# Two depthwise convolutions moved from VectorE to TensorE in the opening of a conv-attention kernel

## The chip, the cores and the metric

The kernel runs on one core of one Trainium2 chip, in one launch, in f32. The metric is the time of one execution on the device in microseconds (us); lower is better. The core has TensorE (PE; weight loads are shown apart as PEld), VectorE (DVE), ScalarE (ACT), GpSimd (POOL) and SyncE (SP, which here only issues DMAs), and 16 DMA engines.

## The reference, cut to what matters

Eight images of 384 channels and 32 x 32 positions pass through two layers. The first normalises each position over its channels, and feeds the result to a selective state-space scan (16 states, forwards and backwards over the 1024 positions) and to a local branch. The second is causal attention with 6 heads and a feed-forward part with binarized weights. The change touches two depthwise convolutions of the first layer: a causal one of 4 taps on one half of the input projection, once in each direction, and a 3x3 one on the normalised image.

```python
xn = rmsnorm(x, norm_w)                        # over channels
u, z = split(xn @ in_proj_w.T)
uc = causal_depthwise_conv(u, conv1d_w)        # 4 taps; once forwards, once on the flipped sequence
u  = silu(uc + conv1d_b)
dt, Bm, Cm = split(u @ x_proj_w.T)
delta = softplus(dt @ dt_proj_w.T + dt_proj_b)
h[t] = exp(delta[t] * A) * h[t-1] + delta[t] * u[t] * Bm[t]     # 384 channels x 16 states
y[t] = sum_n(h[t] * Cm[t]) + u[t] * D ;  y *= silu(z)
conv  = depthwise_conv_3x3(xn, dw_w)           # padding 1
local = sigmoid(conv + dw_b) * xn
x = x + res_scale * (scale_mod * out_proj(y_fwd + y_bwd) + local)
```

## The kernel before, in words

Channels lie on the 128 partitions, in NC = 3 blocks `c`; the 1024 positions lie along the free dimension and are worked on in two halves `h` of 512, which is one PSUM bank. The stages of an image are `before_scan` (everything up to the operands of the scan), the scan itself, and `attention` with `feed_forward`. Images are taken in ORDER = 0, 1, 2, 3, 5, 6, 4, 7.

**before_scan.** It loads the image into `xn` (one of six buffers of the pool `big`, each 3 x 1024 f32 a partition), normalises it (L329), and then, for each channel block: `in_proj` makes `up` and `z` (24 matmuls, L336, copied out at L343); `conv` makes the causal convolution in a PSUM bank, forwards and backwards and for both halves: ACT writes the first tap (L352), DVE adds three more, each as one `scalar_tensor_tensor` that multiplies a shifted view of `up` with a column of `vec` (the weights, one column a tap) and adds it in place (L362), and ACT adds the bias on the way out to `u` (L363); the step `gates` makes the 3x3 convolution with `local`, in two PSUM banks: ACT writes the middle tap (L373), DVE adds eight (L383), each on a window of the picture (31 or 32 columns by 15 or 16 rows). In `gates` ACT then runs silu over `u` and `z` (L423) and tanh over the two banks (L442), with loads of its function tables around them (L446 and others); this order on ACT is pinned. DVE forms the local branch (L449, L452) and the sum of both directions (L427). `project` multiplies `u` with the small weights (L476, L487). After the third block, 12 `delta` steps make the scan's operands (L507 on PE, L510 to L513 on ACT, L514 to L517 on DVE) and write them to memory. For image 0 alone `gates` is cut in two: silu of `u` stays in place, the local branch goes to a list of later steps.

**The scan.** 768 units, 96 an image, each of two states of one block, direction and half. A unit runs through `s_row` (loads of the rows of B and C broadcast over the partitions, tile `bc`), `s_first` (POOL multiplies into `g`, L564; seven buffers), `s_scan` (ACT makes the decay `da`, L577, two PSUM banks; DVE scans, L582, two instructions; POOL keeps the carry, L587, and multiplies with C, L588) and `s_sum` (PE adds up the states by eight transposing matmuls, L598, into one PSUM bank `y`). `s_gate` ends a half of a block (L625 to L640). `s_first` runs two units ahead of `s_scan`, `s_sum` one behind it.

**The order.** The steps of the stages carry weights in us; `spread_over` interleaves lists of steps in proportion to them, and that is the program order. A scheduler then sets the order on each engine ahead of time, by priority and by what is ready; each engine runs its queue in that order. At the start `before_scan` of image 0 runs alone (`begin`). Then the 96 units of image 0 (`first`) run beside the list `beside`: the local branch of image 0, `before_scan` of image 1, the binarizing of `w1` and `w2` (loads into `big`, L205; L223 to L254), and `before_scan` of images 2 and 3. Everything up to there is called the opening here. After it the remaining units run beside attention and feed-forward of one image after the other (its first product is L667), and `before_scan` of the last four images stands beside feed-forward. PSUM has eight banks: `y` 1, `da` 2, `s` 2, `pt` 2, `av` 1; `before_scan` takes its banks from `s` and `pt` in turn.

Of the kernel before, what the change touches and what calls it, by code (L numbers as in the profile page):

```python
# [11 lines left out]
AF = mybir.ActivationFunctionType  # L12
ALU = mybir.AluOpType
# [4 lines left out]
P = 128  # L18
B, C, H, W = 8, 384, 32, 32
L = H * W  # L20
NC = C // P
# [5 lines left out]
DCONV = 4  # L27
# [16 lines left out]
ORDER = (0, 1, 2, 3, 5, 6, 4, 7)  # L44
# [3 lines left out]
V_NORM, V_CW, V_CB, V_DTB, V_D, V_DW, V_DWB, V_BP, V_B2, V_ALOG = 0, 1, 5, 6, 7, 8, 17, 18, 19, 20  # L48
# [4 lines left out]
def kernel(  # L53
# [16 lines left out]
    nc = tc.nc  # L70
# [32 lines left out]
    def half(h):  # L103
        return slice(h * HB, (h + 1) * HB)
# [23 lines left out]
    vec = ctile("vec", [P, NC, NV])  # L128
# [25 lines left out]
    ident = ctile("ident", [P, P])  # L154
# [147 lines left out]
                    )  # L302


    def before_scan(b, tags, emit, later=None):

        st = {}
        turns = itertools.cycle(tags)

        def bank_of(name):  # L310
            return bank(name, next(turns))
# [33 lines left out]
        def conv(c, d, h):  # L345

            acc = bank_of(f"u{d}_{b}_{c}_{h}")
            up = st["up", c]
            for s in range(DCONV):
                w = vec[:, c, V_CW + DCONV - 1 - s : V_CW + DCONV - s]  # L350
                if s == 0:
                    nc.scalar.activation(acc, up[:, half(h)], AF.Copy, scale=w)  # L352
                    continue
                lo, hi = h * HB, (h + 1) * HB
                if d == 0:
                    t0, t1 = max(lo, s), hi
                    tap = up[:, t0 - s : t1 - s]
                else:
                    t0, t1 = lo, min(hi, L - s)
                    tap = up[:, t0 + s : t1 + s]  # L360
                to = acc[:, t0 - lo : t1 - lo]
                nc.vector.scalar_tensor_tensor(to, tap, w, to, ALU.mult, ALU.add)  # L362
            nc.scalar.activation(  # L363
                st["u", d, c][:, half(h)], acc, AF.Identity, bias=vec[:, c, V_CB : V_CB + 1]
            )

        def local(c, h):

            acc = bank_of(f"loc_{b}_{c}_{h}")
            r0, rows = h * (HB // W), HB // W  # L370
            img = acc.rearrange("p (i j) -> p i j", j=W)
            src = st["xn"][:, c, :].rearrange("p (i j) -> p i j", j=W)
            nc.scalar.activation(  # L373
                acc, st["xn"][:, c, half(h)], AF.Copy, scale=vec[:, c, V_DW + 4 : V_DW + 5]
            )
            for k in range(9):
                di, dj = k // 3 - 1, k % 3 - 1
                if k == 4:
# [4 lines left out]
                nc.vector.scalar_tensor_tensor(  # L383
                    to,
                    src[:, i0 + di : i1 + di, j0 + dj : j1 + dj],
                    vec[:, c, V_DW + k : V_DW + k + 1],
                    to,
                    ALU.mult,
                    ALU.add,
                )  # L390
            return acc

        def weights_of(c):
# [9 lines left out]
        for c in range(NC):  # L403
# [29 lines left out]
            def gates(c=c, silus=silus, sum_of_us=sum_of_us):  # L433
                st["xc"] = mtile(f"xc_{b}_{c}")
                load(st["xc"], x[b, chunk(c), :])
                accs = [local(c, h) for h in range(NH)]
                with tc.high_priority(offset=60):
                    us = [st["u", 0, c], st["u", 1, c]] if later is None else []
                    silus(us + [st["z", c]])
                    for h in range(NH):  # L440
                        pin(
                            nc.scalar.activation(  # L442
                                accs[h], accs[h], AF.Tanh, scale=0.5, bias=dwbh[:, c : c + 1]
                            )
                        )
                    pin(nc.scalar.preload_act_table_set(LOG_EXP))  # L446
                for h in range(NH):
                    acc, xc = accs[h], st["xc"][:, half(h)]
                    nc.vector.scalar_tensor_tensor(  # L449
                        acc, acc, 1.0, st["xn"][:, c, half(h)], ALU.add, ALU.mult  # L450
                    )
                    nc.vector.scalar_tensor_tensor(xc, acc, rsh, xc, ALU.mult, ALU.add)  # L452
# [624 lines left out]
    def steps_of(stage, *args):  # L1077
        out = Steps()
        stage(*args, out)
        return out  # L1080


# [1 line left out]
    per, ahead = len(units) // B, 3  # L1084
    first = slots(-AHEAD - 2, per + 1)
    others = slots(per + 1, len(units) + 1)
    beside = Steps()
# [85 lines left out]
```

## Time and profile before

| | |
|---|---|
| median of 10 runs | 5253.6 us (5227.14 to 5259.9) |
| profiled execution | 5256.14 us, span 5254.3 us, mean granted clock 0.865 |
| PE busy | 4173.4 us, 79% of the span, 16458 matmuls |
| DVE busy | 3562.1 us, 68% |
| ACT busy | 2725.3 us, 52% |
| POOL busy | 3669.4 us, 70% |
| DMA | 1199.86 MB, mean 228 GB/s |
| L564 and L588 on POOL | 768 each, 1827.8 and 1817.9 us |
| L383 on DVE (3x3 taps) | 384 instructions, 257.7 us, mean 724 ns |
| L362 on DVE (causal taps) | 288 instructions, 201.3 us, mean 745 ns |

The profile is one execution. Its page gives the busy time of each engine, the span in 40 equal slices (busy tenths, PE's granted clock and DMA's share), the costliest groups of instructions, and DMAs. Behind the page stand views of the trace: a timeline (start, length, engine, line, operation, output and inputs, count; in brackets the idle time before it and what ended it), waits (engine and line, what it waited for, us in total, times, the longest), and windows (busy time of each engine in a stretch). PE's busy time is modelled and overlaps in pipelined matmuls. L-numbers are lines of the kernel before.

### The profile page before, as it was taken

To read this page: it belongs to the slowest core of one execution; us is meant where nothing else is said; L and a number is where in the kernel's file an instruction comes from. 1 tells how busy PE (TensorE), PEld (TensorE's weight loads), DVE (VectorE), ACT (ScalarE), POOL (GpSimd) and SP (SyncE) were. 2 spreads that over 40 slices of the span, in tenths; PEclk is the share of its full clock that TensorE was granted. 3 is DMA by queue.
4 is the path that set the end of the run, shared out by engine and by line. 5 is a ranking of instruction groups with operands and counts; after the bars stand their busy time and mean duration, and the time that the engine had idled before them with its cause. 6 is when DMAs were issued, how large, how long until landed. Compare 5 with 4: busy or idle time off the path is not lost.

```text
span 5254.3 us, 52624 instructions
## 1 busy us (share of the span) xinstructions
PE 4173.4 (79%) x16458; PEld 2199.2 (42%) x16458; DVE 3562.1 (68%) x4249; ACT 2725.3 (52%) x4914; POOL 3669.4 (70%) x1932
## 2 busy tenths in 40 slices
PE   5465566889787888777887788888888888888899
PEld 2233233444344444434444344443444544444444
DVE  6998887667786657776677766677666665666422
ACT  4665554455653555645556445565355363454434
POOL 0477675977777877759876697867788987877700
PEclk7667676989888899889899789998889998999989
DMA  6878688757678667686676876766966866667500
GB/s 226 277 242 281 225 266 274 246 182 266 212 245 293 211 216 244 216 292 222 229 256 212 269 269 207 237 236 218 308 222 219 273 220 226 212 205 239 190 29 25
DMA packets 625121, 1199.86 MB, mean 228 GB/s; under 512 B 44440, under 2 KB 103240, under 8 KB 624840
## 3 DMA queue, kind: packets, MB, share of 16 engines
q1 hardware_dynamic: 615328, 1180.34, 67.1%
q10 hardware_dynamic: 9512, 16.15, 0.9%
q8 instruction: 130, 2.13, 0.2%
q14 instruction: 151, 1.24, 0.1%
HBM read 1030.65 MB, written 165.68 MB: 228 GB/s over the span
## 4 chain that ended last, share of the span: by engine, by line
POOL 32%; issue 20%; DVE 12%; PE 11%; DMA 8%; ACT 3%; SPq 1%; POOLq 0%; DVEq 0%; ACTq 0%
POOL g L564 18%; POOL g L588 13%; DMA bc<-rows 5%; DVE g L582 5%; PE yp L1000 2%; PE s L753 2%; DVE loc L383 1%; PE av L839 1%; DVE u L362 1%; PE y L598 1%; PE qp L697 1%; DVE dp L515 1%; PE pt L825 1%; POOL carry L587 1%; ACT h L980 1%
## 5 line engine op out<-in xcount | busy, mean ns | idle before, releaser
L564 POOL TENSOR_TENSOR g<-ud,bc 128x1024 f32<-128x1024 f32 x768 | 1827.8, 2380 | 842.9 <-PE y L598 431.8
L588 POOL TENSOR_TENSOR g<-g,bc 128x1024 f32<-128x1024 f32 x768 | 1817.9, 2367 | 318.3 <-issue 158.0
L577 ACT ACTIVATE da<-dl,amat 128x512 f32<-128x512 f32 x1536 | 1058.0, 692 | 1637.8 <-DVE g L582 1594.9
L582 DVE TENSOR_TENSOR_SCAN g<-da,g 128x512 f32<-128x512 f32 x768 | 906.4, 1211 | 560.3 <-POOL g L564 523.1
L598 PE MATMUL y<-ident,g 128*128 128x128 f32 x6144 | 965.3, 305 | 384.5 <-POOL g L588 361.1
L582 DVE TENSOR_TENSOR_SCAN g<-da,carry,g 128x512 f32<-128x512 f32 x768 | 955.7, 1272 | 424.2 <-POOL g L564 402.1
L598 PEld LDWEIGHTS y<-ident,g 128*128 128x128 f32 x6144 | 792.6, 157 | 819.9 <-POOL g L588 501.6
L753 PE MATMUL s<-k,q 64*128 64x512 f32 (+3 forms) x1152 | 461.8, 600 | 178.9 <-ACT pr L774 141.5
L773 DVE TENSOR_REDUCE nm<-s 128x1 f32<-128x512 f32 (+3 forms) x576 | 300.4, 545 | 263.9 <-PE s L762 202.1
L774 ACT ACTIVATE pr<-s,nm 128x512 f32<-128x512 f32 (+3 forms) x576 | 329.0, 574 | 150.7 <-DVE nm L773 144.0
L839 PE MATMUL av<-ptn,v 128*64 128x512 f32 (+3 forms) x1152 | 367.7, 543 | 28.8 <-DVE o L851 22.7
L955 PE MATMUL hp<-t,w 128*128 128x512 f32 x720 | 338.4, 615 | 37.9 <-DMA w<-w1s 24.4
L336 PE MATMUL in<-xn,win 128*128 128x512 f32 x576 | 296.8, 660 | 65.3 <-ACT up L343 35.6
L825 PE MATMUL pt<-ident,pr 128*128 128x128 f32 x1728 | 311.7, 305 | 35.6 <-ACT ptn L829 27.0
L1000 PE MATMUL yp<-h,w 128*128 128x512 f32 x720 | 326.5, 612 | 2.7 <-DMA w<-w2s 2.7
L829 ACT COPY ptn<-pt 128x512 f32<-128x512 f32 (+3 forms) x576 | 259.2, 479 | 127.0 <-PE pt L825 124.6
L753 PEld LDWEIGHTS s<-k,q 64*128 64x128 f32 x1152 | 161.8, 205 | 338.7 <-ACT pr L774 220.2
L825 PEld LDWEIGHTS pt<-ident,pr 128*128 128x128 f32 x1728 | 212.1, 154 | 168.1 <-ACT ptn L829 76.1
L697 PE MATMUL qp<-t,wqk 128*128 128x512 f32 x576 | 266.6, 611 | 13.6 <-DVE t L300 13.6
L383 DVE SCALAR_TENSOR_TENSOR loc<-xn,vec,loc 128x496 f32<-128x496 f32 (+3 forms) x384 | 257.7, 724 | 4.2 <-ACT loc L373 4.1
L362 DVE SCALAR_TENSOR_TENSOR u<-up,vec,u 128x512 f32<-128x512 f32 (+3 forms) x288 | 201.3, 745 | 31.5 <-ACT u L352 31.2
L955 PEld LDWEIGHTS hp<-t,w 128*128 128x128 f32 x720 | 134.8, 196 | 193.6 <-issue 151.6
(154 smaller groups left out, 4539.5 us busy)
## 6 DMA issues: line engine op xcount, KB each, us to landing
bc<-rows SPq DMA_DIRECT2D x1536, 512.0 KB, 5.1
t<-st SPq DMA_DIRECT2D x63, 512.0 KB, 6.1
su<-u SPq DMA_DIRECT2D x48, 512.0 KB, 4.6
du<-su SPq DMA_DIRECT2D x96, 256.0 KB, 5.1
sdl<-du SPq DMA_DIRECT2D x96, 256.0 KB, 2.8
sud<-du SPq DMA_DIRECT2D x96, 256.0 KB, 3.4
ud<-sud SPq DMA_DIRECT2D x96, 256.0 KB, 5.7
dl<-sdl SPq DMA_DIRECT2D x96, 256.0 KB, 5.7
```

Of the source, the lines that this page charges most:

```text
L564: pin(nc.gpsimd.tensor_tensor(g, ud, sst.pop(("bc", 0, u.name)), ALU.mult))
L577: nc.scalar.activation(da, sst["dl", u.b, u.c, u.part], AF.Exp, scale=amat[:, u.c, n : n + 1])
L582: nc.vector.tensor_tensor_scan(gi[:, ::step], da[:, ::step], gi[:, ::step], first, ALU.mult, ALU.add)
L588: pin(nc.gpsimd.tensor_tensor(g, g, sst.pop(("bc", 1, u.name)), ALU.mult))
L598: nc.tensor.matmul(out=y[:, j, :], lhsT=g[:, i, chunk(j)], rhs=ident, is_transpose=True, start=(opens and i == 0 and j == 0), stop=(closes ...
L697: nc.tensor.matmul(out=qp, lhsT=st["wqk"][:, c, o : o + P], rhs=st["xn"][:, c, half(h)], start=(c == 0), stop=(c == NC - 1),)
L753: nc.tensor.matmul(out=ss[e][:, : k1 - k0], lhsT=st["q"][rows_of(e), c, chunk(qi)], rhs=st["k"][rows_of(e), c, k0:k1], start=True, stop=(k ...
L774: nc.scalar.activation(pr, s, AF.Exp, bias=m, accum_out=rs[:, i, e, kb : kb + 1])
L825: nc.tensor.transpose(pt[:, chunk(i)], st["pr", c, g, i, e][:, chunk(j)], ident)
L839: nc.tensor.matmul(out=av[rows_of(e), cols], lhsT=st["v"][:, j, hd * HD : (hd + 1) * HD], rhs=st["ptn", j, e][:, cols], start=(j % QT == 0 ...
L955: nc.tensor.matmul(out=hp, lhsT=st["w1"][:, c, chunk(m % 2)], rhs=st["xn"][:, c, half(h)], start=(c == 0), stop=(c == NC - 1),)
L1000: nc.tensor.matmul(out=yp, lhsT=st["w2", k // 6][:, k % 6, :], rhs=st["h", k // NC][:, k % NC, half(h)], start=(k == 0), stop=(k == NF - 1),)
```

## The change

For the first four images of ORDER (all of the opening) both convolutions are done on PE. Ahead of everything, 39 diagonal matrices are made, one for each of the 13 taps and 3 channel blocks: POOL multiplies the 128x128 identity with the tap's column. They lie in two tiles of the pool `big` (eight taps fit in one), which are held until the last tap has been used. A tap is then one f32 matmul of its diagonal with the shifted view, added up in the PSUM bank that DVE used before; the whole first or middle tap opens the sum, so ACT's first write goes too. ACT still reads the bank as before. The last four images keep the old way. Nothing else is changed; numbers of buffers and the weights of the steps are the same.

```diff
-    def before_scan(b, tags, emit, later=None):
+    def before_scan(b, tags, emit, later=None, diags=None):
...
             for s in range(DCONV):
-                w = vec[:, c, V_CW + DCONV - 1 - s : V_CW + DCONV - s]
-                if s == 0:
+                k = V_CW + DCONV - 1 - s
+                w = vec[:, c, k : k + 1]
+                if s == 0 and diags is None:
                     nc.scalar.activation(acc, up[:, half(h)], AF.Copy, scale=w)
                     continue
...
-                nc.vector.scalar_tensor_tensor(to, tap, w, to, ALU.mult, ALU.add)
+                if diags is None:
+                    nc.vector.scalar_tensor_tensor(to, tap, w, to, ALU.mult, ALU.add)
+                else:
+                    nc.tensor.matmul(out=to, lhsT=diags(c, k), rhs=tap,
+                        start=(s == 0), stop=(s == DCONV - 1), skip_group_check=True)
...
-            nc.scalar.activation(
-                acc, st["xn"][:, c, half(h)], AF.Copy, scale=vec[:, c, V_DW + 4 : V_DW + 5]
-            )
-            for k in range(9):
+            if diags is None:
+                nc.scalar.activation(
+                    acc, st["xn"][:, c, half(h)], AF.Copy, scale=vec[:, c, V_DW + 4 : V_DW + 5]
+                )
+            for k in (4, 0, 1, 2, 3, 5, 6, 7, 8):
...
+                tap = src[:, i0 + di : i1 + di, j0 + dj : j1 + dj]
+                if diags is None:
+                    nc.vector.scalar_tensor_tensor(
+                        to, tap, vec[:, c, V_DW + k : V_DW + k + 1], to, ALU.mult, ALU.add)
+                else:
+                    nc.tensor.matmul(out=to, lhsT=diags(c, V_DW + k), rhs=tap,
+                        start=(k == 4), stop=(k == 8), skip_group_check=True)
...
+    taps = list(range(V_CW, V_CW + DCONV)) + list(range(V_DW, V_DW + 9))
+    where, fit = {}, L // P
+    for k in range(0, len(taps), fit):
+        t = btile(f"diag_{k}").rearrange("p c (i q) -> p c i q", q=P)
+        for c in range(NC):
+            for i, tap in enumerate(taps[k : k + fit]):
+                nc.gpsimd.tensor_scalar(
+                    t[:, c, i, :], ident, vec[:, c, tap : tap + 1], None, ALU.mult)
+                where[c, tap] = t[:, c, i, :]
+
+    def diags(c, tap):
+        return where[c, tap]
...
-    before_scan(ORDER[0], ("s", "pt"), begin, beside)
+    before_scan(ORDER[0], ("s", "pt"), begin, beside, diags)
     run(begin)
-    beside += steps_of(before_scan, ORDER[1], ("s", "pt"))
+    beside += steps_of(before_scan, ORDER[1], ("s", "pt"), diags=diags)
...
     for b in ORDER[2 : 1 + ahead]:
-        beside += steps_of(before_scan, b, ("s", "pt"))
+        beside += steps_of(before_scan, b, ("s", "pt"), diags=diags)
```

More of the change, by code (lines that the diff above doesn't have):

```diff
@@ L361, in conv @@
                 to = acc[:, t0 - lo : t1 - lo]
-                nc.vector.scalar_tensor_tensor(to, tap, w, to, ALU.mult, ALU.add)
+                if diags is None:
+                    nc.vector.scalar_tensor_tensor(to, tap, w, to, ALU.mult, ALU.add)
+                else:
+                    nc.tensor.matmul(
+                        out=to,
+                        lhsT=diags(c, k),
+                        rhs=tap,
+                        start=(s == 0),
+                        stop=(s == DCONV - 1),
+                        skip_group_check=True,
+                    )
             nc.scalar.activation(
@@ L372, in local @@
             src = st["xn"][:, c, :].rearrange("p (i j) -> p i j", j=W)
[L373 to L376 removed]
+            if diags is None:
+                nc.scalar.activation(
+                    acc, st["xn"][:, c, half(h)], AF.Copy, scale=vec[:, c, V_DW + 4 : V_DW + 5]
+                )
+            for k in (4, 0, 1, 2, 3, 5, 6, 7, 8):
                 di, dj = k // 3 - 1, k % 3 - 1
[L378 removed]
+                if k == 4 and diags is None:
                     continue
@@ L382, in local @@
                 to = img[:, i0 - r0 : i1 - r0, j0:j1]
[L383 to L390, printed above, removed]
+                tap = src[:, i0 + di : i1 + di, j0 + dj : j1 + dj]
+                if diags is None:
+                    nc.vector.scalar_tensor_tensor(
+                        to, tap, vec[:, c, V_DW + k : V_DW + k + 1], to, ALU.mult, ALU.add
+                    )
+                else:
+                    nc.tensor.matmul(
+                        out=to,
+                        lhsT=diags(c, V_DW + k),
+                        rhs=tap,
+                        start=(k == 4),
+                        stop=(k == 8),
+                        skip_group_check=True,
+                    )
             return acc
@@ L1075, in run, with steps_of @@
             f()
-    def steps_of(stage, *args):
+    def steps_of(stage, *args, **kwargs):
         out = Steps()
-        stage(*args, out)
+        stage(*args, out, **kwargs)
         return out
@@ L1086 @@
     others = slots(per + 1, len(units) + 1)
+    taps = list(range(V_CW, V_CW + DCONV)) + list(range(V_DW, V_DW + 9))
[5 more added lines that the diff above has]
+                nc.gpsimd.tensor_scalar(
+                    t[:, c, i, :], ident, vec[:, c, tap : tap + 1], None, ALU.mult
+                )
+                where[c, tap] = t[:, c, i, :]
+    def diags(c, tap):
+        return where[c, tap]
     beside = Steps()
     begin = Steps()
-    before_scan(ORDER[0], ("s", "pt"), begin, beside)
+    before_scan(ORDER[0], ("s", "pt"), begin, beside, diags)
     run(begin)
-    beside += steps_of(before_scan, ORDER[1], ("s", "pt"))
+    beside += steps_of(before_scan, ORDER[1], ("s", "pt"), diags=diags)
     beside += steps_of(binarize, w1, w1s, NC, FF, 2, "w1")
```

## The prediction, made before the changed kernel had run

> **What bounds the kernel now.** I read the page's 40 slices first, then windows of the first millisecond, then POOL's timeline, gap by gap. A slice is 131 us.
>
> ```profile
> PE   5465566889787888777887788888888888888899
> DVE  6998887667786657776677766677666665666422
> POOL 0477675977777877759876697867788987877700
> PEclk7667676989888899889899789998889998999989
> ```
>
> Over the whole run no engine is full, but the stages differ. In slices 2 to 6 DVE stands at 8 to 9 tenths and PE at 4 to 6, at a clock of 6 to 7 tenths; from slice 8 on PE has 7 to 9 tenths and DVE, but for the last, 5 to 7. The first seven slices (917 us) are about the opening that the change touches: `before_scan` of image 0 by itself, then images 1, 2 and 3 beside the scan of image 0. The windows show it in finer grain (PE, PEld, DVE, ACT, POOL, then PE's clock, the DMA share and GB/s):
>
> ```profile
> core 0: us, PE busy (x) PEld busy (x) DVE busy (x) ACT busy (x) POOL busy (x), PEclk, DMA share, GB/s
> 150.00:200.00 50.00, 10.78 (x22) 4.47 (x20) 50.00 (x78) 34.36 (x46) 5.09 (x5) 0.57 0.83 296
> 200.00:250.00 50.00, 32.18 (x98) 16.78 (x98) 45.57 (x58) 32.13 (x45) 37.14 (x21) 0.82 0.76 259
> 250.00:300.00 50.00, 32.11 (x102) 16.82 (x102) 45.63 (x55) 30.75 (x43) 40.68 (x21) 0.73 0.77 258
> 300.00:350.00 50.00, 29.66 (x106) 15.31 (x106) 42.43 (x54) 32.14 (x45) 40.50 (x24) 0.80 0.74 253
> 900.00:950.00 50.00, 43.12 (x154) 22.77 (x155) 31.69 (x33) 23.38 (x37) 46.75 (x24) 0.97 0.93 319
> ```
>
> At 150 to 200 us the scan should start; DVE is busy for all of it, POOL and PE hardly. 200 to 350 is the convolution part of image 1. The last row, just behind the opening, shows what PE, POOL and DMA can do together. Who holds POOL, which sets the pace of the scan:
>
> ```profile
> POOL carry L587 <- DVE g L582: 82.4, 8, 49.7
> 273.69 9.62 DVE L383 SCALAR_TENSOR_TENSOR loc<-xn,vec,loc 128x496 f32<-128x496 f32 x15
> 277.89 2.40 POOL L564 TENSOR_TENSOR g<-ud,bc 128x1024 f32<-128x1024 f32 x1
> 286.86 2.45 DVE L582 TENSOR_TENSOR_SCAN g<-da,carry,g 128x512 f32<-128x512 f32 x2
> 289.44 2.35 POOL L588 TENSOR_TENSOR g<-g,bc 128x1024 f32<-128x1024 f32 x1 [9.16 <-issue]
> ```
>
> One wait of 49.7 us is the scan's start: the first scan runs at 150.57 us, the second at 192.43, and between them DVE runs 32.3 us of L383, the 3x3 convolution of image 0. The other lines are the pattern of the convolution parts: a run of L383 (here 15 in a row, 9.62 us), behind it the scan of DVE, and POOL without work from 280.3 to 289.4. Between such gaps POOL repeats L588 every 4.87 us (213.67, 218.54, 223.42), which is full. There is one gap for each channel block of images 1 to 3: 8.1, 9.2, 9.3, 12.1, 6.5, 15.9, 10.3, 9.5 and 9.0 us, in sum 89.8 us. POOL's other gaps lie in the `delta` parts between (350 to 450, 590 to 660, 810 to 880), end mostly at `bc` loads, and I leave them as they are. So in this stage the wait that ends last is DVE's, and the convolutions are in it.
>
> **What a matmul costs.** PE's rows give two prices:
>
> ```profile
> 33.62 0.19 PEld L336 LDWEIGHTS in<-xn,win 128*128 128x128 f32 x1 [0.26 <-issue]
> 34.05 0.19 PEld L336 LDWEIGHTS in<-xn,win 128*128 128x128 f32 x1 [0.24 <-issue]
> 182.53 5.01 PE L261 MATMUL ms<-sq_n,onesc 128*128 128x512 f32 x6 [31.56 <-DVE xc L452]
> ```
>
> With the clock up, weight loads follow each other at 0.43 us, one for each f32 matmul of 512 columns, so a tap costs 0.43 us. After PE had idled 31.56 us, six took 5.01 us, 0.84 each. The group's mean (660 ns for L336) is not the price: the spans of matmuls that follow each other overlap.
>
> The Trainium skill, "FP8 and Floating Point Precision", TensorE Precision Notes, says that true FP32 makes four passes through the array, and "TensorE: Matmul & The Clock Gate" gives 2.4 GHz for the warm clock; as an estimate that is 512 x 4 / 2.4 GHz = 0.85 us a tap, twice the spacing in the trace, and speaks against the change: put into the sum below it makes 102 x 0.85 = 87 us of PE work an image, 161 with what is there, 191 us at the rate used there, and so 3 x 41 - 28 = 95 us lost, 5349. The trace decides, and everything else here goes by its 0.43.
>
> **The change part by part.** *Removed from DVE:* in four images 192 instructions of L383 and 144 of L362. Their busy time in the opening by windows is 126.5 and 99.2 us, so 226 us of the 736 us that DVE is busy in the first 900. *Removed from ACT:* the first tap of each sum, L373 x24 and L352 x48, 16.6 + 32.4 = 49 us.
>
> *Added to PE:* each image has 12 half rows of 4 taps and 6 half pictures of 9, so 102 matmuls; four images 408, or 408 x 0.43 = 175 us at full clock (343 us at 0.84). Does PE have room? In 200 to 350 its work in full-clock time is 32.18 x 0.82 + 32.11 x 0.73 + 29.66 x 0.80 = 73.5 us; 102 x 0.43 = 43.9 come on top, 117 us. At the rate of 900 to 950 (43.12 x 0.97 / 50 = 0.84) this takes 140 us, against 150 now. POOL's own bound for the 27 units in these 150 us is 27 x 4.87 = 131. Giving back the gaps whole would make it 120.
>
> *Sum for images 1 to 3:* so each gains 10 us if PE sets the pace, 18 if POOL does, 30 if the gaps just vanish. I take 15, between the first two because both engines would be near full and PE takes its queue in order: 45 us. The DVE work of the same steps that stays (L427, L449, L452: 3.9 us in the gap at 283 to 287) is one reason not to take more.
>
> *The scan's start:* of DVE's 50 us between 150 and 200, 32.3 are L383; PE is idle there (10.8 us busy) and can take the 54 taps of image 0 in 23 to 45 us beside it. DVE keeps the steps of `delta`, which feed the scan anyway. I take 28 us; bounds 0 (were the chain of `delta` and ACT to end as late) and 33.
>
> *Image 0's causal convolution (first 100 us).* Per channel block 16 taps, 6.9 us (13.4 cold), against 12 of L362 at 0.75 = 9 us plus 4 of ACT; but they now stand in the same queue as the input projection (11.1 us for 24). PE is idle after each projection until the silus end, so I take 0; bounds 9 us gained to 21 lost for the three blocks.
>
> *The 39 diagonals on POOL.* No row shows this form. The nearest, POOL's select on 128x128, took 0.29 us: 11 us from 8.5 us, where `vec` lands; the first tap is wanted at 36 us. Were each as long as POOL's 128x1024 product (2.36 us), the four that the first block needs would end at 18 us and the 24 of all causal taps at 65, before the third block's at 86. Cost 0; POOL has nothing else until 134 us, which is its cover.
>
> *Two of six big buffers.* The diagonals hold them until the last tap near 800 us; four are left for the pictures `xn` and for binarizing w1 and w2. The loads of `xn` for images 2 and 3 are issued at 176 and 180 us and first needed near 422 and 652, so they can wait; binarizing will stretch from 20 to 135 us into the next part, where DVE now has room. Cost 0, at most 10 us.
>
> *The new queueing.* On PE, 18 taps in a row (7.7 us, cold 15) stand ahead of the scan's y transposes L598, and those free `g`, for which POOL's L564 waits. `g` has 7 buffers and about four units are under way, so two or three units of 4.87 us cover it. A tap group also waits for a PSUM bank, and whatever stands behind it on PE waits too: now L336 waits so for L452 in 3 places, 9.6 us. I take 5 us lost; bounds 0 and 40.
>
> Sum: 28 + 45 - 5 = 68 us gained. The profiled execution took 5256.14 us (span 5254.3), 2.5 above the median, so 5256.1 - 68 = 5188 for it, and on the median 5253.6 - 68 = 5186 us. Everything behind the opening keeps its work and moves forward as a whole.
>
> **Rivals.** *Only the start is gained.* The gaps stay but change owner: POOL waits for `bc` rows (already 62.7 us in 13 waits in the opening, and 0.93 share of DMA at the pace of 900 to 950), or DVE's L449 stands in its queue for tanh, which stands for PE. Then 28 us: 5226. *Nothing measurable.* `delta`'s chain holds the start and the gaps change owner: near 5250. *Slower: PE becomes the bound of the opening.* It needs 117 us of full-clock work an image. If clock and waits leave it a rate r, that takes 117/r; with the 28 us from the start, r = 117/(150 + 9) = 0.74 is the point from which it loses. Now r is 0.49 in these parts, behind the opening 0.84. At 0.65 an image takes 180 us: 3 x 30 - 28 = 62 us lost, 5316. For it: strict order, bank waits, a clock of 0.73 to 0.87. Against it: the clock reaches 0.97 where PE has work, and the taps of a group depend on nothing new. *It does not do what it says*, if a strided picture row costs PE more than 0.43: that would show as the same loss.
>
> **How the numbers follow.** Forecast 0.58, only the start 0.19, nothing 0.07, slower 0.16. About 0.2%, 10 us, is what a measurement here can tell from no change. Faster 0.58 + 0.19 = 0.77, same 0.07, slower 0.16. The low end takes the whole start (33), all gaps (90) and 20 us of the earlier causal part and of ACT: 5110. The high end takes in the no-change case and a little more, 5262; most of the slower case is left out.
>
> **What would show it.** In the profile after: L383 and L362 only 192 and 144 times, DVE at 5 to 7 tenths and PE at 7 or more with a clock of 8 to 9 in slices 2 to 6; the wait of 49.7 us under 25; POOL's gaps at the gates under 5 us; attention's first step (L667), now at 878 us, near 810. It is wrong if the first slices show PE at 8 to 9 with POOL's waits for y at the head, if `bc` heads them, or if POOL's gaps stay near 10 us with DVE idle in them.

## The result: slower by 0.28%, and the profile after

The changed kernel took 5258.1 us (median; 5246.8 to 5267.7), against 5242.8 us for the kernel before on the same chips. The ratio is 1.0028, 95% interval 1.0017 to 1.0039: about 15 us slower. The forecast was 68 us faster. The time lies inside the range given, 5110 to 5262, and on the other side of no change. The profiled execution took 5263.27 us, its span 5261.4 us, at a mean granted clock of 0.895 (0.865 before). L-numbers below are those of the changed kernel: L367 are the causal taps on PE, L402 the 3x3 taps, L583 and L607 POOL's two products of a unit, L617 the transposing matmuls into `y`, L539 the stores of `delta`.

First the slices of the page:

```profile
PE   7897988888787888778887788888888888888899
DVE  3656557566786657776677766686766665666522
POOL 1476666977686876759876698767688987877700
PEclk9897888899888889889898789898889999999989
```

The work moved as it was meant to: in slices 2 to 6 DVE fell from 8 or 9 tenths to 5 or 6, and PE rose from between 4 and 6 to between 7 and 9. POOL, which sets the pace of the scan, did not gain. The windows of 200 to 350 us, the convolution part of image 1 (columns as in the prediction):

```profile
200.00:250.00 50.00, 49.05 (x147) 24.16 (x147) 28.08 (x30) 23.20 (x34) 35.36 (x20) 1.00 0.93 316
250.00:300.00 50.00, 49.99 (x168) 25.28 (x167) 20.94 (x20) 29.53 (x39) 35.08 (x17) 1.00 0.78 261
300.00:350.00 50.00, 48.40 (x160) 24.17 (x159) 23.11 (x23) 25.37 (x34) 34.82 (x22) 1.00 0.64 224
```

PE is busy for 147.4 of 150 us at a granted clock of 1.00: it is full, and no clock is left to be had. DVE fell from 133.6 to 72.1 us. POOL went from 118.3 to 105.3 us. POOL's waits from 190 to 890 us (engine, line, what it waited for: us in total, times, longest):

```profile
POOL g L583 <- PE y L617: 112.3, 26, 11.0
POOL g L583 <- DMA bc<-rows: 50.2, 9, 11.0
POOL g L607 <- DMA bc<-rows: 38.2, 8, 8.4
POOL carry L606 <- DVE g L601: 7.1, 1, 7.1
```

Before, `carry` led with 82.4 us, and the waits for `y` came to 5.5 us in 2:

```profile
POOL g L564 <- PE y L598: 5.5, 2, 4.2
```

So the gaps behind DVE are gone and gaps behind PE have come. PE's queue around one of them, from the timeline, and POOL's answer:

```profile
240.52 3.59 PE L367 MATMUL u<-up,diag 128*128 128x512 f32 x8
243.94 1.04 PE L617 MATMUL y<-ident,g 128*128 128x128 f32 x8
244.81 7.03 PE L367 MATMUL u<-up,diag 128*128 128x512 f32 x16
251.69 1.03 PE L617 MATMUL y<-ident,g 128*128 128x128 f32 x8
252.56 3.59 PE L367 MATMUL u<-up,diag 128*128 128x512 f32 x8
255.98 1.04 PE L617 MATMUL y<-ident,g 128*128 128x128 f32 x8
256.86 14.98 PE L402 MATMUL loc<-xn,diag 128*128 128x512 f32 x36
271.68 1.04 PE L617 MATMUL y<-ident,g 128*128 128x128 f32 x8
...
259.74 2.35 POOL L607 TENSOR_TENSOR g<-g,bc 128x1024 f32<-128x1024 f32 x1
272.79 2.36 POOL L583 TENSOR_TENSOR g<-ud,bc 128x1024 f32<-128x1024 f32 x1 [10.70 <-PE y L617]
```

A unit's eight transposes take 1.04 us, but they stand between groups of causal taps of 3.6 to 7.0 us and behind the 18 taps of a 3x3 sum, 14.98 us. POOL runs out of free `g` there and waits 10.70 us, until the `y` at 271.68 has been made: about as long as before, when DVE held it up at the gates.

**Why: a matmul here leaves two records.** The code has 192 causal matmuls and 216 of the 3x3 taps. The groups (busy us, mean ns | idle before):

```profile
L402 PE MATMUL loc<-xn,diag 128*128 128x496 f32 (+3 forms) x432 | 182.9, 583 | 4.4 <-DVE du L535 4.4
L367 PE MATMUL u<-up,diag 128*128 128x512 f32 (+3 forms) x384 | 169.8, 594 | 2.8 <-ACT up L344 2.8
```

One channel block of image 0, from the timeline:

```profile
49.45 13.88 PE L367 MATMUL u<-up,diag 128*128 128x512 f32 x32
```

Each count is twice the code's, and the page's total went from 16458 to 17274 records, 816 for 408 matmuls. In the block, 4 sums of 4 taps are 16 matmuls, with 32 records in 13.88 us, 0.87 us a matmul. The spacing of 0.43 us in the trace of before was that of two halves of one matmul. It could have been read there: the L336 group counts 576, and 8 images of 3 blocks with 2 outputs, 2 halves and 3 chunks of channels are 288 matmuls. (The description of the kernel above says 24 matmuls a block for `in_proj`; they are 12, with 24 records.)

### The profile page after: what moved, and what is told of

It is laid out like the page before. It is cut to its first block, busy times and chain, and to the rows that moved or that the text cites. A ratio compares the mean times of both kernels' runs of the same rounds, so it can differ in the third digit from the quotient of the medians.

```text
span 5261.4 us, 53903 instructions
## 1 busy us (share of the span) xinstructions
PE 4421.8 (84%) x17274; PEld 2316.8 (44%) x17274; DVE 3348.1 (64%) x3908; ACT 2692.4 (51%) x4856; POOL 3689.3 (70%) x1971
## 4 chain that ended last, share of the span: by engine, by line
POOL 33%; issue 22%; PE 19%; DVE 11%; DMA 10%; ACT 4%; SPq 1%; POOLq 0%; ACTq 0%; DVEq 0%
POOL g L583 18%; POOL g L607 15%; DMA bc<-rows 7%; DVE g L601 4%; PE loc L402 2%; PE y L617 2%; PE in L337 2%; PE s L772 2%; PE yp L1019 2%; PE u L367 2%; PE qp L716 1%; DVE dp L534 1%; PE av L858 1%; PE hp L974 1%; DVE loc L398 1%
## 5 line engine op out<-in xcount | busy, mean ns | idle before, releaser
L583 POOL TENSOR_TENSOR g<-ud,bc 128x1024 f32<-128x1024 f32 x768 | 1824.5, 2376 | 938.7 <-PE y L617 542.7
L607 POOL TENSOR_TENSOR g<-g,bc 128x1024 f32<-128x1024 f32 x768 | 1817.7, 2367 | 278.1 <-issue 100.6
L617 PE MATMUL y<-ident,g 128*128 128x128 f32 x6144 | 925.7, 297 | 221.9 <-POOL g L607 192.3
L617 PEld LDWEIGHTS y<-ident,g 128*128 128x128 f32 x6144 | 770.4, 153 | 634.9 <-issue 314.5
L858 PE MATMUL av<-ptn,v 128*64 128x512 f32 (+3 forms) x1152 | 367.7, 546 | 28.2 <-DVE o L870 22.7
L337 PE MATMUL in<-xn,win 128*128 128x512 f32 x576 | 279.8, 631 | 47.1 <-ACT up L344 35.6
L844 PEld LDWEIGHTS pt<-ident,pr 128*128 128x128 f32 x1728 | 212.7, 154 | 166.9 <-ACT ptn L848 75.7
L1019 PEld LDWEIGHTS yp<-h,w 128*128 128x128 f32 x720 | 138.6, 196 | 176.0 <-issue 169.6
L526 PE MATMUL dp<-xd,wdt 25*128 25x512 f32 x192 | 140.3, 899 | 74.4 <-DVE du L535 68.5
```

What stands on the lines that cost most here:

```text
L337: nc.tensor.matmul(out=mp, lhsT=st["win", c][:, k, i, :], rhs=st["xn"][:, k, half(h)], start=(k == 0), stop=(k == NC - 1),)
L583: pin(nc.gpsimd.tensor_tensor(g, ud, sst.pop(("bc", 0, u.name)), ALU.mult))
L607: pin(nc.gpsimd.tensor_tensor(g, g, sst.pop(("bc", 1, u.name)), ALU.mult))
L617: nc.tensor.matmul(out=y[:, j, :], lhsT=g[:, i, chunk(j)], rhs=ident, is_transpose=True, start=(opens and i == 0 and j == 0), stop=(closes ...
L844: nc.tensor.transpose(pt[:, chunk(i)], st["pr", c, g, i, e][:, chunk(j)], ident)
L858: nc.tensor.matmul(out=av[rows_of(e), cols], lhsT=st["v"][:, j, hd * HD : (hd + 1) * HD], rhs=st["ptn", j, e][:, cols], start=(j % QT == 0 ...
```

## Experiments

My theory after the result: a tap costs 0.86 us, so PE is the bound of the convolution parts; and image 0's causal part, a chain by itself, is longer on PE than on DVE. Rivals: the big buffers that the diagonals hold; something that holds back the scan even if taps are free. A third rival was not held fixed in any run: the scheduler lays out the steps of each kernel anew, and that order can cost or win some us by itself. "Unit k" is the start of POOL's second product of the k-th unit; image 1's convolution part lies about units 1 to 25 and its `delta` part behind. The last time is attention's first product. The starts are from one profiled execution of each kernel; the ratio is to the kernel before.

| kernel | unit 1 | unit 9 | unit 25 | unit 33 | unit 97 | attention | ratio, 95% interval |
|---|---|---|---|---|---|---|---|
| before | 194.1 | 247.9 | 342.2 | 405.3 | 848.0 | 877.9 | 1 |
| after | 184.1 | 240.5 | 348.7 | 405.9 | 851.0 | 886.8 | 1.0028 [1.0017, 1.0039] |
| causal_only | 179.4 | 252.9 | 342.9 | 416.9 | 858.3 | 889.0 | 1.0021 [1.0007, 1.0035] |
| causal_f32r | 156.8 | 230.3 | 323.3 | 390.8 | 824.6 | 857.6 | 0.9944 [0.9922, 0.9966] |
| local_only | 159.7 | 231.9 | 320.1 | 388.0 | 816.7 | 846.3 | 0.9936 [0.9917, 0.9955] |
| hold | 158.1 | 254.6 | 354.0 | 417.7 | 857.8 | 887.4 | 1.0014 [1.0000, 1.0027] |
| img0_local | 157.7 | 229.1 | 339.3 | 399.8 | 839.8 | 868.6 | 0.9994 [0.9979, 1.0009] |
| one_tap | 145.2 | 212.2 | 303.4 | 382.9 | 825.1 | 854.4 | 0.9966 [0.9952, 0.9980] |
| local8 | 163.8 | 219.0 | 299.5 | 373.1 | 802.5 | 832.7 | 0.9919 [0.9892, 0.9947] |
| local5 | 166.9 | 221.9 | 318.9 | 392.3 | 829.8 | 860.0 | 0.9970 [0.9952, 0.9987] |
| local8_d2 | 160.6 | 223.2 | 304.7 | 370.9 | 781.3 | 818.1 | 0.9889 [0.9859, 0.9919] |

What a kernel of the table has won or lost by attention's first product it keeps, to within 26 us: from there to the end of the span these kernels take 4350 to 4376 us. So the larger differences are made in the opening; one of a few us can't be placed by a single profile of each kernel. Unit 1 alone is a poor mark of the scan's start. `hold`, which leaves image 0's convolutions on DVE, has it 36 us earlier than before, but unit 2 then waits for DVE's scan:

```profile
158.14 2.35 POOL L607 TENSOR_TENSOR g<-g,bc 128x1024 f32<-128x1024 f32 x1
207.47 0.18 POOL L606 COPY carry<-g 128x2 f32<-128x2 f32 x1 [44.21 <-DVE g L601]
```

At unit 9 `hold` is 7 us late. I go by unit 9 for the start.

**Half of the change, and the price taken away.** `local_only` has the 3x3 taps on PE and the causal ones on DVE, `causal_only` the other way round.

```diff
-    before_scan(ORDER[0], ("s", "pt"), begin, beside, diags)
+    before_scan(ORDER[0], ("s", "pt"), begin, beside, None, diags)   # causal, 3x3; images 1 to 3 alike
```

> Only the 3x3 convolution of the first four images is on PE, the causal one stays on ACT and DVE. Price theory: PE has 54 taps of about 0.83 us an image, 45 us in place of 88, and image 0's run in PE's idle time; 15 to 60 us faster than before. Queue theory: six sums an image in place of 18, so a third of the loss: about 5 us slower than before or level. Buffer theory: as slow as the changed kernel.

> Only the causal convolution of the first four images is on PE, the 3x3 stays on ACT and DVE (two big buffers are not needed, one is held). Price theory: 48 taps of 0.86 us, 41 us an image; image 0's come in a chain of their own, 13.9 us a block against some 10, so the start is 10 to 15 us later, and DVE's runs of 3x3 taps with POOL's gaps behind them stay: 0 to 25 us slower than before. Queue theory: 12 of the 18 sums, so two thirds of the changed kernel's loss, 5 to 12 us slower. Buffer theory: half the buffers, half the loss.

`local_only` was faster by 0.64%, `causal_only` slower by 0.21%. The useful half is the 3x3 convolution, which in image 0 lies beside other work; the causal one alone turns a gain into a loss. POOL's waits for `y` in the opening fall with the taps on PE: 112.3 us in the change, 33.1 in `local_only`, 12.0 in `causal_only`, and 3.7 in `one_tap` below. `causal_f32r` is `causal_only` with the same sums, waits and buffer, but its diagonals and `up` are written as float32r, and every tap of an even number of columns (36 of 48 an image) is multiplied in that type. The 3x3 taps, with rows of 31 columns, were not tried in it.

```diff
+                    rt = F32 if (t1 - t0) % 2 else mybir.dt.float32r
...
-                        lhsT=cdiags(c, k),
-                        rhs=tap,
+                        lhsT=cdiags(c, k).bitcast(rt),
+                        rhs=tap.bitcast(rt),
```

> As the kernel with only the causal convolution on PE, but 36 of its 48 taps an image (those with an even number of columns) are matmuls in the reduced f32r type, on diagonals and an up that are rounded to it when written; the odd ones stay f32. So the taps' values are rounded, nothing is left out. Price theory: an f32r tap is one record, 0.22 to 0.43 us in place of 0.86, PE loses 16 to 23 us an image, and the chain of image 0 is 4 to 6 us a block shorter: 10 to 30 us faster than with f32 taps. Queue and buffer theories: sums, waits and the held buffer are the same, so within 8 us of it, near 5255.

It took 5218.1 us, 0.9944: by the two ratios some 40 us less than `causal_only` (1.0021), more than the 10 to 30 expected, for a change of the price alone. Of this, 23 us are there at unit 9 and 31 at attention, so most of it is the chain of image 0, and the rest came behind unit 25. The same 16 taps of image 0's first block in the timeline of `causal_only` and in that of `causal_f32r`:

```profile
47.68 13.88 PE L367 MATMUL u<-up,diag 128*128 128x512 f32 x32
```

```profile
47.39 6.76 PE L371 MATMUL u<-up,diag 128*128 128x512 f32 x20
```

Groups of `causal_f32r` by shape:

```profile
L371 PE MATMUL u<-up,diag 128*128 128x512 f32 x120 | 40.7, 457 | 0.0
L371 PE MATMUL u<-up,diag 128*128 128x511 f32 x48 | 24.4, 590 | 0.0
```

Of 512 columns there are 120 taps, now one record each; the 24 taps of 511 columns stay f32 and have 48. In the 16 taps four are f32: 6.76 - 4 x 0.86 = 3.3 us for twelve, about 0.28 us each. The price of a tap, and through it the length of image 0's chain, are shown as causes.

**The buffers.** `hold` makes all 39 diagonals and holds both big buffers, but leaves the convolutions as before, apart from the first taps of the last opening image's third block.

```diff
-                if s == 0 and diags is None:
+                if s == 0 and (diags is None or c < NC - 1):   # 3x3 alike; the other taps stay on DVE
```

> The kernel before, with the 39 diagonals built on POOL and the two big buffers held until the end of the opening; of the taps only the first ones of the last image's third block (6 matmuls) are on PE, all others stay on ACT and DVE. Price theory: within 10 us of before, since neither the buffers nor the building are on the path. Buffer theory: slower than before by 10 to 30 us, with the first image's normalisation and the scan's start late.

It lost 0.14%, 7 us, with an interval that reaches from 0 to 14; attention came 9.5 us later. So did image 0's first input projection; here it is in the kernel before and in `hold`:

```profile
27.74 13.33 PE L336 MATMUL in<-xn,win 128*128 128x512 f32 x24 [8.07 <-DVE xn L329]
```

```profile
37.24 12.35 PE L337 MATMUL in<-xn,win 128*128 128x512 f32 x24 [4.67 <-DVE xn L330]
```

So what `hold` lost may be all in this late start, which comes from the order of DVE's steps, and not in the buffers later on. `img0_local` has image 0's 3x3 taps alone on PE, with two buffers, whose diagonals no later image uses.

```diff
-    beside += steps_of(before_scan, ORDER[1], ("s", "pt"), cdiags=None, diags=diags)
+    beside += steps_of(before_scan, ORDER[1], ("s", "pt"), cdiags=None, diags=None)   # images 2, 3 alike
```

> Only the 3x3 convolution of image 0 is on PE (54 matmuls, about 45 us, where PE waits); images 1 to 3 and all causal taps stay on ACT and DVE. Price theory: the start of the scan gains what the prediction put there, 15 to 28 us, and POOL's nine gaps behind DVE's 3x3 taps stay. SP-queue theory: part of it is given back at the next delta part; 5 to 20 us faster than before.

Its scan is 19 us ahead of the kernel before at unit 9, of which 3 are left at unit 25; attention comes 9 us earlier than before and 19 earlier than in `hold`, and the time is level (0.9994), where 5 to 20 us were expected. `local8` lays eight taps, which fit in one big buffer, on PE and leaves the ninth to DVE; `local8_b` is the same kernel again beside `local8_2buf`, where the same eight lie four to a tile and hold two.

```diff
-    taps = list(range(V_CW, V_CW + DCONV)) + list(range(V_DW, V_DW + 9))
+    taps = [V_DW + k for k in (4, 0, 1, 2, 3, 5, 6, 7)]
-    where, fit = {}, L // P
+    where, fit = {}, L // P // 2      # local8_2buf alone
```

> The 3x3 convolution of the first four images with eight taps on PE and the ninth on DVE, behind them; the causal one stays on ACT and DVE. Nine times three diagonals needed two big buffers, eight times three fill one. PE has 48 matmuls an image in place of 54, DVE six more instructions of 0.73 us. Buffer theory: 4 to 12 us faster than the kernel with all nine on PE. Price theory alone: within 5 us of it, about 5208.

> local8 once more, on the chip and beside the runs of the kernel before that local8_2buf and local5 are compared on: 0.990 to 0.9935, as before.

> As local8, with the eight taps' diagonals laid four to a tile, so that two big buffers are held and not one; every instruction on PE, DVE and POOL is the same. If the buffer made local8 better than local_only: ratio near 0.9936 or 0.994. If it was the ninth tap, moved back to DVE: near 0.992, as local8.

`local8` came to 0.9919 and `local8_b` to 0.9920 [0.9900, 0.9939], `local8_2buf` to 0.9937 [0.9916, 0.9957]. Attention comes 7 us later with the second buffer (840.6 against 833.3), and the first input projection 2.6 us later (36.9 against 34.3); in the times alone the intervals overlap. The buffers, with the new order at the start, are a term of some 7 us, not the cause of the miss.

**How many taps PE should have.** `local5` puts five of the nine taps on PE.

```diff
+    taps = [V_DW + k for k in (4, 0, 1, 2, 3)]
...
+                if diags is None or k > 4:        # on DVE
```

> As local8, but five of the nine 3x3 taps on PE and four on DVE (one big buffer). PE loses 18 taps an image more, 18 x 0.86 = 15.5 us; DVE gets 18 more of 0.67 us, 12 us. If PE still sets the pace of the convolution parts with eight taps: 0.988 to 0.990. If POOL, DVE and the bc rows do: 0.992 to 0.996, no better than local8.

0.9970: worse than eight taps. The case in which PE still sets the pace of `local8` fell. The windows of `local8`, then of `local5`:

```profile
200.00:250.00 50.00, 43.54 (x160) 23.20 (x159) 41.65 (x46) 35.89 (x50) 44.16 (x21) 0.97 0.98 322
250.00:300.00 50.00, 45.52 (x170) 24.80 (x170) 42.26 (x50) 36.94 (x51) 47.29 (x29) 0.94 0.89 304
```

```profile
200.00:250.00 50.00, 42.14 (x146) 21.44 (x145) 47.83 (x57) 39.26 (x56) 39.62 (x20) 0.97 0.90 295
250.00:300.00 50.00, 36.48 (x128) 18.74 (x127) 43.24 (x52) 30.56 (x42) 41.41 (x25) 0.90 0.85 287
```

With eight taps PE, DVE and POOL all stand near 42 to 47 of 50 us; POOL's 91 us in these 100 are what the forecast wanted (77.8 before). With five, DVE is back at 47.8 in the first window and POOL falls to 81.

**Taps almost free.** `one_tap` leaves out three of four causal taps and eight of nine 3x3 taps of the first four images, on every engine; the first of each sum is on PE. `one_tap_1buf` makes its six diagonals alone, in one buffer.

```diff
-                else:
+                elif s == 0:      # and k == 4 for the 3x3
```

> Left out: three of the four causal taps and eight of the nine 3x3 taps of the first four images (the first tap of each sum stays on PE), so PE has the same 18 sums an image, each with its PSUM bank, its place in the queue and its readers, but 18 matmuls in place of 102. Price theory (a f32 tap costs PE two records of 0.43 us, 0.86 in all, and PE is full in the convolution parts): 40 to 90 us faster than before, POOL's waits for y in the opening gone. Queue theory (the sums' bank waits and PE's strict order cost, not the matmuls): within 15 us of the changed kernel. Buffer theory (the two big buffers and the building of the diagonals cost): not faster than before by more than 20 us.

> As one_tap (three of four causal taps and eight of nine 3x3 taps of the first four images are left out), but only the six diagonals that it uses are made, so that one big buffer is held and not two. If the held buffers are a good part of what one_tap is short of the forecast: ratio near 0.993 (some 20 us better than one_tap's 0.9966). If hold's price is the whole of it (two buffers, 0.14%): 0.995 to 0.9965. If POOL's waits for bc rows are what is left: still 0.996 to 0.997, with these waits above 150 us between 190 and 860 us.

With nearly all of both convolutions gone, only 0.34% is gained (18 us, where the price theory had asked for 40 to 90), or 0.43% with one buffer (0.9957 [0.9940, 0.9974]). `local8`, which does more work on PE, DVE and ACT, gains more (0.9919, and 0.9920 when run again). No run here explains that; the order of the steps, which differs between the two, may. Unit 25 starts 39 us earlier than before, unit 33 only 22: the `delta` part between takes 79 us instead of 63. The longest waits of POOL and of SP's queue in `one_tap` from 190 to 860 us:

```profile
POOL g L583 <- DMA bc<-rows: 163.1, 30, 14.3
...
SPq L539 <- DVE du L535: 99.2, 33, 11.3
```

The timeline of SP, which issues in order, and of POOL in that part:

```profile
327.44 1.13 SPq L110 DMA_DIRECT2D du<-su  x2
337.47 0.32 SPq L539 DMA_DIRECT2D sdl<-du  x1
339.50 0.32 SPq L539 DMA_DIRECT2D sud<-du  x1
339.91 0.39 SPq L110 DMA_DIRECT2D bc<-rows  x1
...
344.39 2.35 POOL L583 TENSOR_TENSOR g<-ud,bc 128x1024 f32<-128x1024 f32 x1 [5.47 <-DMA bc<-rows]
```

SP issues nothing from 328.6 to 337.5, because the store `sdl` waits for DVE's part of `delta`; the load of `bc` stands behind it, and POOL waits for those rows. Were that the cause, the stores on another queue should free it. The five `_actq` kernels issue the stores of the opening's images (in `after_actq`, `one_tap_actq`, `local_actq` = `local_only`, and `local8_actq`; `before_actq` is the kernel before) on ACT's queue.

```diff
-                nc.sync.dma_start(out=t, in_=du[:, i, :])
+                (nc.sync if diags is None else nc.scalar).dma_start(out=t, in_=du[:, i, :])
```

> As the kernel with one tap a sum (three of four causal taps and eight of nine 3x3 taps of the first four images are left out), and the 24 stores of delta's results of each of these images are issued by ACT's queue in place of SP's. Queue-of-SP theory (with the convolutions gone, POOL waits 163 us for bc rows in the opening because their loads stand in SP's queue behind stores that wait for DVE's delta steps): POOL's wait for bc falls below 90 us and the kernel gets 15 to 40 us faster than with one tap alone, about 5190 us. Rival (bandwidth: the loads are late because the DMA engines are full): the wait stays at 120 us or more and the time within 10 us of one tap alone. ACT pays some 8 us of issues an image either way.

> The 3x3 convolution of the first four images on PE (nine taps), the causal one on ACT and DVE, and delta's stores of these images on ACT's queue in place of SP's. SP-queue theory: POOL's wait for bc rows in the opening (153 us in the kernel without this step) falls by 40 us or more, 10 to 30 us faster than it, near 5190. Rival (bandwidth, or ACT's in-order queue now stands where SP's stood): level or slower, 5210 to 5230.

> Eight of nine 3x3 taps of the first four images on PE, one on DVE, and delta's stores of these images on ACT's queue. SP-queue theory: the 155 us in which POOL waits for bc rows in the opening fall under 60, but ACT's queue now holds da back behind the stores, as in the other two kernels with this step: 5 to 20 us faster than without it, near 5180. If ACT's waits cost all of it: level.

> The changed kernel with delta's stores of the first four images on ACT's queue. Price theory: POOL's waits in the convolution parts are for y behind a full PE, which this step does not touch; PE's records in 200 to 350 us stay at 147 us or more of 150, and the time is within 12 us of the changed kernel. SP-queue theory alone (the order of SP and not PE took the gain): 20 us or more faster than it.

> The kernel before with delta's stores of the first four images on ACT's queue. It tells whether this step is worth anything by itself: in the kernel before POOL waits 70 us for bc rows in the opening, but 96 us for DVE's scans. SP-queue theory: the first wait falls by 30 us or more, and DVE, near full, takes most of it: 0 to 15 us faster than before.

`one_tap_actq` 0.9956 [0.9938, 0.9975], `local_actq` 0.9932 [0.9909, 0.9955] and `local8_actq` 0.9908 [0.9878, 0.9937] can't be told from the same kernels with the stores on SP; `before_actq` is level (1.0005 [0.9988, 1.0021]); `after_actq` is slower than the change (1.0072 [1.0046, 1.0099]), by some 23 us where at most 12 were expected. Yet all but `after_actq` reach attention earlier than the same kernel with the stores on SP, by 15 to 31 us: `local8_actq` at 811.8 us, 21 before `local8`, and it then takes 4396 us to the end. Part of that is the spread of single executions (its profiled one took 9 us more than its median); the rest says that what is won in the opening is not always kept. POOL's waits in `one_tap_actq`:

```profile
POOL carry L606 <- DVE g L601: 92.8, 6, 33.9
POOL g L583 <- DMA bc<-rows: 54.8, 11, 11.9
POOL g L607 <- DVE g L601: 28.3, 1, 28.3
POOL g L607 <- DMA bc<-rows: 14.3, 4, 7.2
```

The waits for rows fell from 181 to 69 us, so the stores on SP do hold the rows back; but the scan's wait came to 121 us in their place. ACT forms the decay `da`, for which DVE's scan waits, and its queue now holds the stores. In the longest of these waits, 595 to 629 us, ACT forms one `da` at 607.80 and the next at 626.87, with eight stores and other steps of `delta` between. That the stores hold `da` back is likely; stores and steps were not tried apart. So the `delta` parts seem to have a second limit close behind the first.

**Weights of the steps.** Two runs moved scan units between the parts of `local8`: fewer beside the gates, or fewer beside `delta`.

```diff
-                emit(gates, 14.0)
+                emit(gates, 14.0 if diags is None else 9.0)                  # local8_g9
-                emit(lambda c=c, d=d, h=h: delta(c, d, h), 3.0)
+                emit(lambda c=c, d=d, h=h: delta(c, d, h), 3.0 if diags is None else 1.5)   # local8_d2
```

> As local8, but the weight of the step gates of the first four images is 9 and not 14, so that fewer scan units stand beside the faster convolution parts and more beside the delta parts. If POOL's waits in the delta parts come from too few units there to work on: ratio 0.986 to 0.990, better than local8's 0.992. If the rows are late whatever stands beside (the loads wait behind delta's stores): 0.992 to 0.997, and POOL's waits for bc rows stay above 130 us between 190 and 860 us.

> As local8, but the weight of a delta step of the first four images is 1.5 and not 3, so that fewer units stand beside the delta parts, where the rows come late. If the rows are late because their loads stand among delta's stores: ratio 0.986 to 0.991, waits for bc rows clearly under 130 us. If the weights matter little: 0.991 to 0.994. If it starves POOL instead: 0.994 to 1.0.

`local8_g9` is as `local8` (0.9919 [0.9896, 0.9941]). `local8_d2` is the fastest kernel here, 5179.1 us against 5241.3, 0.9889 [0.9859, 0.9919]; its interval overlaps that of `local8`. Its waits for rows are still 157 us, so the reason that I had given for such a gain is not borne out, and that the weights made it is not settled.

## Why the prediction was wrong, step by step

**The step that failed is the price of a tap**, "so a tap costs 0.43 us". It was 0.86: the spacing that was read is that of two records of one matmul. (So is the cold price, "0.84 each": the six records in 5.01 us are three matmuls, one for each block of channels, at 1.67 us.) The Trainium skill, "FP8 and Floating Point Precision", TensorE Precision Notes, gives true FP32 four passes; with the warm clock of "TensorE: Matmul & The Clock Gate", Part 1, that made the estimate of 0.85 us which the prediction set aside, and the runs agree with it: 0.87 us. In float32r a tap took near a third of that, 0.28 us. A second step failed beside it, what was left out of the sum; it is the last point of the list.

With the right price PE's sum falls into place. Image 1's part needs 73.5 + 102 x 0.86 = 161 us of full-clock work in place of 117. PE delivered 147.4 us in 150 at clock 1.00, a rate of 0.98 and not 0.84, so 161 take 164 us, 14 more than before. Measured, units 1 to 25 took 164.6 us against 148.1 before, 16 us lost, and 14 of them from unit 9 on. Three images and the 28 us of the start would give 3 x 14 - 28 = 14 us lost, about what was measured; but that agreement is luck. The start gave 10 us at unit 1 and 7 at unit 9; image 1's `delta` part gave 6 back (units 25 to 33: 57 us against 63); and units 33 to 97, beside which images 2 and 3 are made ready, took 445 us against 443, so these two images lost next to nothing. At unit 97 the changed kernel is 3 us late and at attention 9; where the rest of the 15 us arises, one profile of each does not show. The price-led case in the prediction, 5349, went wrong by its rate of 0.84: the clock was 1.00 where PE was full.

- *Removed from DVE:* right. L398 and L365, the taps left on DVE, stand 192 and 144 times; DVE's busy time fell by 214 us (226 expected), and the 82.4 us of `carry` waits to 7.1.
- *The scan's start:* the 49.7 us wait is gone, as listed, but unit 9 came 7 us earlier and not 28; attention, listed for 810, came at 887. `img0_local`, where the causal part stays on DVE, shows 19 at unit 9. A gain at the start wasn't worth its size anyway: of those 19 us, 9 reach attention.
- *Image 0's causal part:* taken at 0. A block's 16 taps took 13.88 us on PE, twice the 6.9 of the prediction, against 9 on DVE. `causal_only` shows it as a loss, `causal_f32r` as a gain. In the change `project` of the third block starts at 129.3 us, against 102.9 before. The first input projection also came 9.3 us later (37.04 against 27.74): ten reductions of the binarizing (DVE L223, from 25.96 to 32.2) and a step that waits for its load until 35.8 (L246) now stand in DVE's queue ahead of image 0's normalising, where one reduction did before. The scheduler put them there; I had not expected that it would order other steps anew. `hold` has this too, so it is not an effect of the taps.
- *The diagonals on POOL:* 39 took 22.7 us, 0.58 each, twice the row that I took; cover held.

```profile
L1113 POOL TENSOR_SCALAR diag<-ident,vec 128x128 f32<-128x128 f32 x39 | 22.7, 601 | 1.0 <-DMA vec<-in_vecs 1.0
```

- *Two big buffers:* taken at 0, at most 10. About 7 by `hold`: inside its bound, and of the sign it had, though the late first projection may be all of it; the binarizing, expected to stretch into the next part, moved ahead instead.
- *The new queueing:* taken at 5 (0 to 40). Waits for `y` rose from 5.5 to 112.3 us. The 18 taps ahead of a `y` took 14.98 us where 7.7 were expected, and seven buffers of `g` did not cover that.
- *The rivals:* the slower one came true in mechanism (full PE, the waits for `y` at the head, both listed as signs of a wrong forecast), at a quarter of its price of 62 us. That price had put 117 us of work at a rate of 0.65; it was 161 us at 0.98.
- *Small misreadings:* L564 and L588 stand 25 times each between 200 and 350 us, so POOL's own bound there is 25 x 4.87 = 122 us and not 131, which would have raised the forecast; and in slice 12 DVE stands at 8 tenths. Neither had a part in the failure.
- *What was missing:* with the taps on PE almost free the forecast would still have failed. It left POOL's gaps in the `delta` parts "as they are", but they grew when the parts between became shorter: `one_tap` waits 181 us for rows, the kernel before 70. So even at 0.43 us a tap the sum would have needed this term. What bounds these parts once the stores are moved stays open.

## What to carry to other kernels

Before pricing a matmul from a trace, count its records against the code's calls: an f32 matmul of 512 columns here is two records, and one spacing is half its cost. When work moves from one engine to another, look for the point where both are about equally full: eight 3x3 taps on TensorE with the causal ones left on VectorE gave 0.8% and nine gave 0.6%, which can't be told apart; five gave 0.3%, all nine and the causal ones lost 0.3%. And follow a gain past the part that is made faster to the next one, and to the end: a scan that starts 19 us earlier here was worth 9 us at attention, and in the time too little to be told from nothing.

## What the runs showed of the hardware

An f32 matmul of 512 columns shows as two loads and two matmul records 0.43 us apart at full clock; in float32r it is one record, at about 0.28 us. The granted clock rose with PE's load: 0.73 to 0.82 before at about 32 of 50 us busy, 1.00 after at 49 of 50, in the same 150 us. GpSimd's multiplication of a 128x128 f32 tile with a column took 0.58 us, where a select of the same size took 0.29.
